# New written orders for the opening and the first feed-forward stage of a macaron block, with earlier halves of the first tiles and later biases

## The chip, the cores and the metric

The kernel runs on one core of one Trainium2 chip. The number that counts is the time of one execution on the device in microseconds (us); the kernel before takes 1006.35 us, the median of three runs (1004.93 to 1006.83). The engines that matter are TensorE (PE, matrix products and transposes; PEld is its weight load), VectorE (DVE), ScalarE (ACT), GpSimd (POOL), and the queue of SyncE (SP), which only issues DMA transfers. Each engine takes its instructions in the order in which they were written; an instruction that has to wait holds up all that stand behind it on its engine.

## The reference

The input is 4096 rows of 256 numbers (2 x 2048 x 256, float32). With `ffn` the quantised feed-forward block, the reference computes

```
x = x + 0.5 * ffn(layernorm(x))
x = x + attention(layernorm(x))
x = x + 0.5 * ffn(layernorm(x))

ffn(x):   gate = q(x) @ q(w_gate).T          # 256 -> 704
          up   = q(x) @ q(w_up).T            # 256 -> 704
          return q(silu(gate) * up) @ q(w_down).T   # 704 -> 256
q(v):     blocks of 16 along the last axis; scale = max(max|block| / 6, 1e-12)
          v / scale rounded to the grid 0, .5, 1, 1.5, 2, 3, 4, 6 (with sign), times scale
attention(x): q, k, v = x @ Wq.T + bq, x @ Wk.T + bk, x @ Wv.T + bv   (512 wide)
          softmax(q k.T / 16) v @ Wo.T + bo, for each of the two sequences of 2048 rows
```

All inputs and the output are float32. The weights of the feed-forward block are quantised in the kernel too, and they are the same for both feed-forward blocks.

## The kernel before

The 4096 rows are 32 tiles of 128 rows, kept on chip in four groups of eight tiles (`xs`, 1 MB each). The kernel has an opening, the first feed-forward stage (FFN0), attention, and the second feed-forward stage (FFN1). Products come in pieces: for tile i, `p{i}` is gate product (PE), silu (ACT), up product (PE), and gate times up (DVE); `b{i}` is the product with w_down (PE) and its addition to x (DVE).

**Opening** (`opening`). It loads the weights and the first group of x, quantises w_gate and w_up in two halves each (`g0 g1 u0 u1`, function `half`) and w_down in two (`d0 d1`, function `down`), folds the projections of attention into two matrices (`f`, function `fold`), measures the layer norms of the first two groups (`n0 n1 n2`), normalises and quantises tiles 0 to 11 in pairs (`x0` to `x5`), makes the products of tiles 0 to 7 (`p0` to `p7`), quantises their hidden rows in pairs (`h0` to `h3`), turns four of these tiles with PE (`t0` to `t3`) and takes them back (`b0` to `b3`). A quantisation is a chain over three engines: DVE takes the largest of each block, scales and inverts it; POOL or DVE multiplies; ACT takes absolute values; DVE rounds in two instructions (lines 426 and 428); POOL or DVE multiplies back (line 430).

Each of these activities is a generator, and each `yield` ends one step. The string `ORDER` lists 261 steps by name; the function `opening` runs them in just that order, and `fence` then ties the instructions of each engine to that order. The planner has no freedom left there: where a name stands in the string decides what stands ahead of it on PE, DVE, ACT, POOL.

**FFN0** (`woven`) is written in the same way by `FFN0_ORDER` (503 steps) for tiles 8 to 31. Here a quantised tensor is turned by a DMA transpose instead of PE. For a pair of hidden tiles, `h{i}` is DVE and ACT work, then a transposing DMA (line 259, SP queue), then one multiplication on POOL (line 261). `s{i}` brings the scales: one PE transpose (`ts`, line 272), an ACT copy (`whole`), a DMA that lays them out (`eight`, line 278), and a DMA that spreads them over the target tile (`hqT<-eight`, line 281). `x{i}` and `y{i}` are the same for four input tiles (`xqT<-eight`). There is a single buffer `eight`: the next line-278 transfer waits until the line-281 transfer before it has landed. All of these are issued by the SP queue in written order. `n3`, `m0`, `m1` are further layer norm statistics, `a0` to `a7` turn the rows of the first sequence for attention, `q` makes its first scores, `t4` to `t7` turn the last hidden tiles of the opening. Attention and FFN1 follow; their order is not touched.

Buffers that the steps share: PE's gate and up products have two PSUM buffers (`p_big`), the products `b{i}`, the weight transposes and the scores have two (`p_acc`). So a new product waits until ACT or DVE has read an older one.

**Loads.** The ACT queue issues the first four tiles of x as one transfer of 512 KB (line 148) and the four biases; the SP queue issues w_gate rows, wq, the other w_gate rows, wk, w_up, wv, wo, the other four tiles of x, w_down, and the remaining groups of x (lines 162 to 187). A row of w_gate is 1 KB; `load_rows` puts row r*128+p on partition p.

## Time and profile before

| | |
|---|---|
| time, median of three runs | 1006.35 us |
| time of the profiled execution | 1006.27 us |
| span of its trace (first to last instruction) | 1004.5 us |
| TensorE clock granted | 1.0 throughout |
| busy: PE / DVE / ACT / POOL | 979.8 / 797.1 / 416.7 / 409.3 us |
| first instruction of DVE on data | 6.17 us |
| first gate product | 30.0 us |
| opening ends (last `b3` addition on DVE) | about 92 us |
| FFN0 ends, attention goes on alone | about 326 us |

The span is split into engines' busy times; an instruction of PE that overlaps the next one is counted to its modelled end, so the idle times between PE rows are better read from the starts of the rows: a gate or up product is eight rows of 0.296 us each from start to start (2.37 us), a product with w_down twelve rows of 0.216 us (2.59 us). Times in the trace count from the start of the span.

### The profile page before, as it was taken

To read this page: it belongs to the slowest core of one execution; us is meant where nothing else is said; L and a number is where in the kernel's file an instruction comes from. 1 tells how busy PE (TensorE), PEld (TensorE's weight loads), DVE (VectorE), ACT (ScalarE), POOL (GpSimd) and SP (SyncE) were. 2 spreads that over 40 slices of the span, in tenths; PEclk is the share of its full clock that TensorE was granted. 3 is DMA by queue.
4 is the path that set the end of the run, shared out by engine and by line. 5 is a ranking of instruction groups with operands and counts; after the bars stand their busy time and mean duration, and the time that the engine had idled before them with its cause. 6 is when DMAs were issued, how large, how long until landed. Compare 5 with 4: busy or idle time off the path is not lost.

```text
span 1004.5 us, 11698 instructions
## 1 busy us (share of the span) xinstructions
PE 979.8 (98%) x4137; PEld 750.0 (75%) x4137; DVE 797.1 (79%) x1324; ACT 416.7 (41%) x745; POOL 409.3 (41%) x451
## 2 busy tenths in 40 slices
PE   5999999999999999999999999999999999999998
PEld 3667766767766888888888888888765666776776
DVE  7999999979753798665688858677978389988896
ACT  4755543343333534353544444343654244233121
POOL 4465132331124595566665555556411102133231
PEclk9999999999999999999999999999999999999999
DMA  9001255442430000000000000000000033665553
GB/s 310 28 1 40 56 113 94 96 106 55 90 88 2 0 1 1 1 1 1 1 1 1 1 1 1 1 1 1 0 1 1 10 79 99 127 136 109 123 115 75
DMA packets 59294, 49.40 MB, mean 49 GB/s; under 512 B 46050, under 2 KB 51171, under 8 KB 58851
## 3 DMA queue, kind: packets, MB, share of 16 engines
q1 hardware_dynamic: 58272, 48.11, 21.3%
q10 hardware_dynamic: 962, 0.53, 0.3%
q8 instruction: 33, 0.54, 0.2%
q14 instruction: 27, 0.21, 0.1%
HBM read 8.46 MB, written 4.19 MB: 13 GB/s over the span
## 4 chain that ended last, share of the span: by engine, by line
PE 80%; DVE 15%; ACT 2%; issue 1%; DMA 1%; SPq 0%; ACTq 0%; DVEq 0%
PE gu L591 23%; PE m L1153 16%; PE ps L1256 13%; PE po L647 12%; PE poa L1202 3%; PE pu L970 3%; PE ps L1224 2%; PE z L1172 2%; PE ps L1016 2%; DVE h L252 2%; PE ps L1033 1%; DVE qh_s L233 1%; PE th L632 1%; DVE h L609 1%; DMA wq_sb<-in_wqT_dram 1%
## 5 line engine op out<-in xcount | busy, mean ns | idle before, releaser
L591 PE MATMUL gu<-wgu,xqT 128*128 128x352 f32 x992 | 306.2, 460 | 2.7 <-issue 0.8
L591 PEld LDWEIGHTS gu<-wgu,xqT 128*128 128x128 f32 x992 | 185.3, 190 | 101.1 <-issue 5.9
L647 PE MATMUL po<-wd,hqT 128*128 128x256 f32 x768 | 174.0, 380 | 0.0
L647 PEld LDWEIGHTS po<-wd,hqT 128*128 128x128 f32 x768 | 144.1, 190 | 26.3 <-issue 2.7
L261 POOL TENSOR_TENSOR hqT<-hqT,qh_t 128x1408 f32<-128x1408 f32 x24 | 74.6, 3109 | 194.7 <-DMA qh_t<-h 154.0
L1153 PE MATMUL m<-st,xn 128*128 128x256 f32 x448 | 132.9, 379 | 0.0
L1256 PE MATMUL ps<-uT,xS 128*128 128x256 f32 x432 | 127.3, 379 | 0.0
L1153 PE MATMUL m<-tw,xn 128*128 128x256 f32 x336 | 99.9, 379 | 0.0
L1128 POOL TENSOR_TENSOR tw<-st 128x256 f32<-128x256 f32 x55 | 46.3, 841 | 129.9 <-PE m L1153 62.0
L1153 PEld LDWEIGHTS m<-st,xn 128*128 128x128 f32 x448 | 84.5, 190 | 11.3
L1256 PEld LDWEIGHTS ps<-uT,xS 128*128 128x128 f32 x432 | 80.9, 190 | 10.9
L605 ACT ACTIVATE h<-gu 128x704 f32<-128x704 f32 x62 | 46.7, 756 | 99.2 <-PE gu L591 95.2
L609 DVE TENSOR_TENSOR h<-h,gu 128x704 f32<-128x704 f32 x62 | 54.3, 878 | 35.0 <-PE gu L591 29.0
L1109 DVE TENSOR_TENSOR st<-st,top 128x1024 f32<-128x1024 f32 x64 | 76.5, 1210 | 2.8 <-PE top L1104 2.7
L1113 ACT ACTIVATE st<-st 128x1024 f32<-128x1024 f32 x64 | 66.7, 1058 | 11.7 <-DVE st L1109 11.5
L1153 PEld LDWEIGHTS m<-tw,xn 128*128 128x128 f32 x336 | 63.8, 190 | 8.6
L1233 DVE TENSOR_TENSOR most<-st,most 128x512 f32<-128x512 f32 x49 | 39.4, 803 | 32.3 <-ACT st L1274 32.3
L1256 PE MATMUL ps<-uT,xT 128*128 128x256 f32 x216 | 64.4, 380 | 0.1
L261 POOL TENSOR_TENSOR xqT<-xqT,qx_t 128x1024 f32<-128x1024 f32 x9 | 20.3, 2258 | 104.9 <-DMA qx_t<-qx_q 62.8
L1266 ACT COPY st<-ps 128x256 f32<-128x256 f32 x54 | 20.1, 373 | 98.6 <-PE ps L1256 98.6
L249 ACT ACTIVATE qh_m<-h 128x1408 f32<-128x1408 f32 x24 | 33.0, 1376 | 56.7 <-DVE h L244 36.9
L1130 POOL TENSOR_TENSOR tw<-st 128x256 f32<-128x256 f32 x55 | 50.0, 910 | 4.3
(234 smaller groups left out, 1625.9 us busy)
## 6 DMA issues: line engine op xcount, KB each, us to landing
hqT<-eight SPq DMA_DIRECT2D x24, 704.0 KB
...
```

The lines of the kernel that those rows point to most:

```text
L261: nc.gpsimd.tensor_tensor(state["dst"], state["dst"], crossed, ALU.mult)
L591: nc.tensor.matmul(out=ps[:, b2, 0:HALF], lhsT=xqT[:, i % XT, kc, :], rhs=wgu[:, kc, ts(which * 2 + b2, HALF)], start=(kc == 0), stop=(kc ...
L605: nc.scalar.activation(h, gate, AF.Silu)
L609: nc.vector.tensor_tensor(h, h, up, ALU.mult)
L647: nc.tensor.matmul(out=po, lhsT=hqT[:, r, :], rhs=right, start=(k == 0), stop=(k == NR - 1))
L1109: nc.vector.tensor_tensor(piece, piece, top, ALU.subtract)
L1113: nc.scalar.activation(piece, piece, AF.Exp, scale=SCALE)
L1128: add(t[:, 0, :], b[:, 0, :], b[:, 1, :], ALU.add)
L1130: add(t[:, 1, :], b[:, 1, :], b[:, 0, :], ALU.add)
L1153: i = nc.tensor.matmul(out=gr.m[k], lhsT=left, rhs=right, start=first, stop=last)
L1233: nc.vector.tensor_tensor(gr.most, piece[:, 1, :], gr.most, ALU.max)
L1256: nc.tensor.matmul(out=out, lhsT=left, rhs=right, start=start, stop=stop, skip_group_check=True)
```

## The change

Four things are changed.

1. `ORDER` and `FFN0_ORDER` hold the same steps in another order. Nothing is added or taken from either.
2. The first four tiles of x come in two transfers of two tiles each, both on the ACT queue.
3. The first halves of w_gate and w_up are loaded with three rows after each other on a partition (3 KB in one piece, row 3p+r on partition p) instead of rows 128 apart; the ACT copies of those halves into `wgu` write with a stride of three to put the columns back. w_up is loaded in two halves and its last rows.
4. The biases leave the ACT queue for the SP queue: bq and bk behind w_gate, bv behind w_up, bo behind w_down. bv is loaded as four rows of 128 numbers, and PE and ACT turn it into a column (one transpose into a `p_big` buffer and one copy), where POOL copied it before.

The choice of one of two buffers in `turned` (attention's rows) was by a count of calls and is now by a fixed list; the list gives the same buffers to the same p as the count did in the order before.

```diff
@@ -33,25 +33,25 @@
 
 
 FFN0_ORDER = """
-t5 x12 n2 n3 x12 x12 n2 n2 n2 m0 t5 x12 x12 n2 p8 p8 t4 x12 t4 n3 n2 x12 n3 p9 y12 n2 p9 p8 y12 m0
-n2 n3 n2 x12 y12 n2 n2 p9 p8 x12 n2 x12 y12 p9 t7 t7 n3 b5 h8 n2 n3 h8 n3 h8 t6 p10 h8 s8 p10 x12
-x12 n2 n2 n2 p11 h8 p11 t6 x16 h8 x16 h8 b5 n3 x16 m0 p11 x16 n3 x16 p11 m0 s8 b4 p10 p10 b7 h10 h10
-n3 b4 x12 p12 s8 x16 s10 x16 p12 m0 x16 h10 s10 h10 n3 p13 p12 p13 s8 x16 s10 p13 x16 h8 p12 p13 y16
-p15 n3 x16 h10 n3 h10 b7 x20 b6 x20 p14 h12 h12 b6 s10 h10 x16 s12 h8 x20 x20 m0 m0 m0 m0 x20 y16
-h12 y16 x20 y16 x20 s12 x20 b9 p15 m0 h10 p14 h12 p15 x16 p14 b9 b8 p14 p15 s12 h14 h14 y20 x20 n3
-m0 p17 h12 h12 s12 p16 h12 h14 p17 s14 b8 m1 h14 p16 s14 p16 n3 p16 h14 h10 p17 s14 n3 h14 p17 s14
-x20 h12 y20 y20 b11 b11 x20 m0 p19 p19 p18 h12 h16 h16 x24 m0 p18 h14 s16 m0 x24 s16 h16 y20 x20 b10
-p19 x24 x24 p18 b12 x20 p19 m0 s16 h16 m0 b10 b13 h16 a1 h14 x24 p18 a0 x24 p20 h14 a0 h18 h18 a1
-s16 b12 s18 m1 s18 x24 a0 p20 a0 m1 p21 s18 h16 x24 b13 h18 p21 x24 m1 h16 y24 p21 h16 p20 p21 p20
-x24 m1 a1 s18 h18 b14 h18 p23 h20 y24 h20 a1 x24 m1 y24 h18 b15 h20 p22 p23 b14 m1 h16 h18 p23 h20
-p22 s20 b16 x24 x28 y24 s20 h18 x24 p23 p22 b15 h20 b17 p24 p22 m1 m1 h18 h22 h20 s20 h22 p25 m1 s20
-x28 p24 m1 b16 h20 p25 s22 p24 s22 h20 h22 p25 x28 b17 h22 s22 h20 x28 x28 x28 a3 a3 a2 q y28 p24
-p25 h22 b20 b20 x28 a2 p26 s22 m1 x28 a2 y28 x28 h22 h22 a3 a2 y28 y28 h24 b18 b19 m1 h24 b18 h22
-x28 b19 x28 p26 a3 p27 x28 p27 h24 p27 h24 p26 m1 p27 m1 p26 m1 s24 s24 x28 h26 b21 a4 p28 p29 h26
-h24 a4 s26 p28 h22 s24 h24 h26 a4 h24 p28 h26 s26 h24 b22 s24 a4 p28 p29 s26 b21 p29 p29 p31 h28 p30
-h26 p30 h28 p31 s28 a7 s26 h26 a5 h28 b23 a7 p31 a5 a7 h24 h28 a7 h26 p31 s28 b23 p30 h26 a5 s28 b22
-a6 b24 p30 a6 h28 h28 b24 h30 a6 q s28 a5 h28 q h30 a6 q s30 h26 h30 b27 h30 s30 h28 b27 b25 h28 b25
-h30 s30 h30 q h30 b28 s30 h30 b29 b28 h30 b29 q b30 b31 b30 b26 b31 b26
+p8 p8 n2 p9 t4 t5 m0 n2 p9 x12 p9 n2 p8 x12 x12 n2 x12 x12 x12 t4 p8 t5 x12 n2 b5 n3 y12 t7 n2 n3
+x12 y12 p9 n2 y12 n2 n3 n2 h8 p10 x12 n2 x12 h8 h8 n2 n2 n3 n3 t7 t6 n2 p11 b7 p10 x12 p10 p11 n2 n2
+n2 h8 s8 y12 x16 m0 x16 b7 x12 p10 m0 p11 s8 t6 m0 x12 s8 b4 p11 h8 h8 x16 h10 p12 x16 p12 h10 x16
+x16 h10 p13 h8 p13 b4 h10 b5 s10 p13 p13 s8 s10 x16 h10 x16 p12 h10 s10 p12 x16 h12 y16 p14 y16 n3
+b6 m0 b6 p15 x16 h8 m0 h12 p14 s10 y16 y16 p14 h12 s12 h8 x16 p15 m0 x16 m0 p14 h10 p15 p15 b9 x20
+x20 x20 x20 h14 b8 x20 h10 n3 s12 n3 x16 h14 p16 m0 h10 x20 b8 m0 h14 p17 y20 m1 h12 x20 p16 h12 p17
+s12 h12 n3 h12 n3 s14 s14 p16 b10 s12 p18 m0 b9 p16 n3 h14 h14 s14 p17 m0 h12 y20 n3 x20 n3 p18 x20
+p17 h16 s14 x20 x20 h16 b11 n3 b11 n3 n3 y20 x20 h12 b10 p19 m0 h14 p19 x24 x24 h16 p19 m0 m1 y20
+s16 m1 s16 x24 p18 h14 s16 h16 p19 p18 b13 h14 m0 x20 h18 h18 h16 b12 x24 x24 p20 m1 x24 s18 h16 p20
+h18 b13 b12 p21 h18 h14 p21 p21 x24 m0 x24 s18 b14 p20 x24 p21 m1 s16 a0 s18 h16 p20 b15 s18 x24 h16
+b15 p23 y24 h18 p23 a0 x24 h16 h20 x28 p23 a0 p22 y24 h20 h18 b14 x24 m1 a1 h20 x28 y24 a1 s20 p23
+h18 x28 y24 p22 h20 b16 a0 s20 a2 b16 m1 p22 p22 s20 x28 x28 a1 x24 h22 h22 x28 m1 h18 h20 a1 a2 x28
+h18 s20 q m1 a3 p25 h22 s22 q s22 m1 m1 h20 h20 p24 b17 h22 s22 p25 b18 p24 a3 h22 b17 h22 p25 p25
+p24 p24 m1 b19 h24 s22 h20 x28 b19 p27 x28 h24 m1 p27 b18 y28 p26 p26 m1 h20 x28 h22 x28 y28 a3 b21
+m1 y28 x28 s24 p27 h24 s24 y28 b20 h24 p26 m1 a3 b20 p27 a4 h22 a4 a2 a7 h24 p26 h22 h26 x28 h24 a4
+a7 h26 h24 b23 h26 a2 h26 p28 p29 p28 p28 b23 p29 p29 h24 p28 s24 p31 s24 s26 a4 h26 a5 p29 s26 p31
+p30 s26 b21 q b22 a7 h28 p30 p30 h28 h26 s28 h28 s26 a7 b22 h24 a6 h28 b24 s28 p31 h26 h28 b24 h28
+h26 p30 q h26 a6 h28 p31 q h30 b27 s28 s28 h30 s30 h28 a5 h30 s30 b27 h28 s30 b25 s30 h30 b28 b25 a6
+a5 b29 h30 h30 h30 h30 b28 a5 b29 q h30 b26 b31 b26 b30 a6 b30 b31
 """
 FFN1_ORDER = """
 n2 h6 n2 t5 t4 p8 t4 t5 h6 n3 p9 h6 s6 p8 n2 p9 n2 n3 s6 n3 p9 n2 p8 n2 n2 n2 h6 p9 n2 p8 n3 h8 p10
@@ -74,14 +74,14 @@
 b30 h31b t31 t31 b30 b29 b31 b29 b31
 """
 ORDER = """
-n0 n0 n0 g0 g0 g0 g0 n0 n0 g0 n0 g1 n0 g1 n0 f n0 g1 g0 n0 f g0 f n0 g1 n0 g0 g1 x1 u1 x0 f x1 u0 x0
-g1 f u0 g0 u1 g1 f f x0 x1 g1 u0 x0 n1 u1 g1 n1 u0 x0 n1 x0 f x1 n1 n1 u1 x1 n1 d1 u0 u1 x1 u0 n2 g1
-f n1 n2 n1 u1 x0 d1 g1 f n1 x0 x1 x0 n1 u1 g0 x0 n1 x1 g0 p0 n1 x3 u1 u0 x2 p1 u1 n2 p0 d0 u1 x3 x1
-u0 u0 x3 d0 d1 n2 d0 d1 d1 u1 p1 n2 x2 n2 u0 n2 x3 u0 x2 d0 x3 x1 n2 x3 x2 n2 p0 x3 x2 n2 d1 x2 d0
-n2 p0 d0 n2 x3 n2 p1 p3 x2 p1 f n2 x2 n2 d0 h0 p3 d1 d0 h0 n2 p2 d1 p2 h0 x3 x4 x3 p3 x4 h0 x4 p3 p2
-x2 p2 x4 x5 x5 h1 d0 x2 x5 p6 p4 x4 h0 h0 p6 p5 h1 x4 h0 p4 d1 x4 h0 x4 h1 p5 p4 p5 h1 h0 h1 x5 p4
-d0 p5 p7 x4 h1 h2 d1 t0 p7 d1 x5 h1 x5 h2 t0 h1 p6 x5 p6 h2 h2 t1 p7 h1 h2 p7 h3 x4 d0 t1 x5 h2 b0
-h3 t2 h3 x5 h3 t2 h2 b1 b0 t3 x5 h2 t3 h3 b1 h3 h3 b2 h2 h3 b3 b2 b3 h3
+n0 n0 g0 g0 g0 n0 g0 n0 n0 n0 g1 g1 n0 g0 g1 n0 n0 f f g1 u0 g0 n0 u0 u0 n0 g0 n0 f g1 u0 u0 g0 g1
+g1 u1 n1 f n1 x0 g1 x1 x0 f n1 u1 n1 x0 g1 n1 u1 u0 u1 n1 x1 f d0 f g0 u1 n2 f x0 n1 x0 u0 n1 x0 x0
+n1 f x0 u1 f g0 n1 d0 x0 u0 g1 x0 g0 n1 g1 u1 n1 d1 u0 x1 n2 x1 x3 p1 p1 u0 n2 x1 u1 x1 n2 u0 p0 d1
+d0 u1 x3 x2 d1 x1 x1 n2 d0 d1 x1 u1 n2 n2 x3 x2 n2 x2 u1 d0 n2 p0 p1 n2 p1 x2 x1 d0 p0 f x3 n2 p3 d1
+p0 d1 x2 n2 p3 d1 d0 x3 x2 x2 n2 p2 x3 p2 p2 x2 n2 h0 x2 n2 x3 x2 x3 x3 n2 p2 h0 x4 d0 x5 d1 p3 x3
+p4 h0 d0 d0 h0 h0 p3 p4 h0 x4 p6 p6 x4 p5 d0 x5 h1 x5 h1 x4 d1 x4 h0 h0 p5 h1 p5 p5 h0 p4 x4 p6 x5
+t0 h1 p4 h2 h2 h1 t1 x4 p7 x5 h1 x4 t1 h2 h1 d1 d1 x4 x4 p7 t0 h1 p6 b1 x5 h1 p7 t2 b1 x5 h2 p7 h3
+h3 x5 h2 x5 h3 h3 t2 b0 b0 t3 b2 h2 h2 h2 h3 t3 h3 h3 b3 h2 h3 b2 b3 x5 h3
 """
 TURNED = 4
 
@@ -145,7 +145,8 @@
 
 
     xs = [const.tile([P, GT, D], FP, tag=f"x{g}", name=f"x{g}") for g in range(NG)]
-    nc.scalar.dma_start(out=xs[0][:, 0:4, :], in_=x_g[0][:, 0:4, :])
+    nc.scalar.dma_start(out=xs[0][:, 0:2, :], in_=x_g[0][:, 0:2, :])
+    nc.scalar.dma_start(out=xs[0][:, 2:4, :], in_=x_g[0][:, 2:4, :])
     w_nat = []
     for name in ("gate", "up"):
         t = wpool.tile([P, NR, D], FP, tag=f"n_{name}", name=f"n_{name}")
@@ -165,24 +166,30 @@
             nc.sync.dma_start(out=t[0:LAST, NR - 1, :], in_=w[(NR - 1) * P:FF, :])
 
     NH = NR // 2
-    load_rows(w_nat[0], w_gate, 0, NH)
+    bq_sb = wpool.tile([P, KE], FP, tag="bq", name="bq_sb")
+    bk_sb = wpool.tile([P, KE], FP, tag="bk", name="bk_sb")
+    bv_sb = wpool.tile([KE, P], FP, tag="bv", name="bv_sb")
+    bo_sb = wpool.tile([P, D], FP, tag="bo", name="bo_sb")
+
+    def load_next(t, w):
+
+        nc.sync.dma_start(out=t[:, 0:NH, :], in_=w[0:NH * P, :].rearrange("(p r) k -> p r k", p=P))
+
+    load_next(w_nat[0], w_gate)
     nc.sync.dma_start(out=wq_sb, in_=wqT.rearrange("(k p) e -> p k e", p=P))
     load_rows(w_nat[0], w_gate, NH, NR)
+    nc.sync.dma_start(out=bq_sb, in_=bq)
+    nc.sync.dma_start(out=bk_sb, in_=bk)
     nc.sync.dma_start(out=wk_sb, in_=wkT.rearrange("(k p) e -> p k e", p=P))
-    load_rows(w_nat[1], w_up, 0, NR)
+    load_next(w_nat[1], w_up)
+    load_rows(w_nat[1], w_up, NH, NR)
+    nc.sync.dma_start(out=bv_sb, in_=bv.rearrange("(c p) -> c p", p=P))
     nc.sync.dma_start(out=wv_sb, in_=wvT.rearrange("(k p) e -> p k e", p=P))
     nc.sync.dma_start(out=wo_sb, in_=woT.rearrange("(k p) e -> p k e", p=P))
     nc.sync.dma_start(out=xs[0][:, 4:GT, :], in_=x_g[0][:, 4:GT, :])
     nc.sync.dma_start(out=wd_nat, in_=w_down.rearrange("(r p) k -> p r k", p=P))
-    bq_sb = wpool.tile([P, KE], FP, tag="bq", name="bq_sb")
-    bk_sb = wpool.tile([P, KE], FP, tag="bk", name="bk_sb")
-    bv_sb = wpool.tile([P, KE], FP, tag="bv", name="bv_sb")
-    bo_sb = wpool.tile([P, D], FP, tag="bo", name="bo_sb")
     nc.gpsimd.memset(bo_sb[P - 32:P, :], 0.0)
-    nc.scalar.dma_start(out=bq_sb, in_=bq)
-    nc.scalar.dma_start(out=bk_sb, in_=bk)
-    nc.scalar.dma_start(out=bv_sb, in_=bv.rearrange("(c p) -> p c", p=P))
-    nc.scalar.dma_start(out=bo_sb[P - 1:P, :], in_=bo.unsqueeze(0))
+    nc.sync.dma_start(out=bo_sb[P - 1:P, :], in_=bo.unsqueeze(0))
     for g in range(1, NG):
         nc.sync.dma_start(out=xs[g], in_=x_g[g])
 
@@ -440,9 +447,11 @@
             ps = weight_bank([P, 4, P], f"wt{which}_{half}_{kc}")
             for r in range(NH):
                 nc.tensor.transpose(ps[:, r, :], t[:, half * NH + r, ts(kc, P)], ident)
-            nc.scalar.copy(
-                wgu[:, kc, ds(which * FF + half * NH * P, n)], ps.rearrange("p r k -> p (r k)")[:, 0:n]
-            )
+            to = wgu[:, kc, ds(which * FF + half * NH * P, n)]
+            if half == 0:
+                nc.scalar.copy(to.rearrange("q (p r) -> q r p", r=NH), ps[:, 0:NH, :])
+            else:
+                nc.scalar.copy(to, ps.rearrange("p r k -> p (r k)")[:, 0:n])
             yield
 
     def down(r):
@@ -477,8 +486,12 @@
                 nc.scalar.activation(
                     nat[name][:, c0 + c, 0:D - 1], ps[:, c, 0:D - 1], AF.Identity, bias=last[:, c:c + 1]
                 )
-            if c0 == 0:
+            if c0 == 0 and bias.shape[0] == P:
                 nc.gpsimd.tensor_copy(nat[name][:, :, D - 1], bias)
+            elif c0 == 0:
+                turned = p_big.tile([P, 2, 512], FP, tag="big", name="bias")[:, 0, 0:KE]
+                nc.tensor.transpose(turned, bias, ident[0:KE, 0:KE])
+                nc.scalar.copy(nat[name][:, :, D - 1], turned)
 
         def matrix(dst, left, right, kc):
             ps = weight_bank([P, D], f"wm{kc}")
@@ -854,7 +867,7 @@
     PLAIN = NP + LAG
     groups = NT // QG
 
-    kept, turns = {}, {"nat": 0}
+    kept = {}
 
     def ones_last(pool, tag, k, shape, last):
 
@@ -882,8 +895,7 @@
 
         def turned(self, p, kt):
 
-            turns["nat"] += 1
-            if turns["nat"] % 2:
+            if p in ((1, 3, 4, 5), (0, 2, 4, 6))[self.b]:
                 nat = ones_last(xp, "xl", None, [P, 4, D], lambda t: t[:, :, D - 1])[:, 0:2, :]
             else:
                 nat = ones_last(kt, "nat", 0, [P, 2, D], lambda t: t[:, :, D - 1])
```

## The prediction

> **What bounds the kernel now.** Read first: the page's busy tenths in 40 slices, then the busy times by stretch (PE, PEld, DVE, ACT, POOL, granted clock, DMA share, GB/s).
>
> ```profile
> PE   5999999999999999999999999999999999999998
> DVE  7999999979753798665688858677978389988896
> ```
>
> ```profile
> 0.00:30.00 30.00, 17.21 (x72) 12.85 (x72) 23.26 (x69) 16.24 (x40) 12.88 (x22) 1.00 0.81 282
> 30.00:92.00 62.00, 59.99 (x262) 42.84 (x263) 59.62 (x99) 36.21 (x60) 37.20 (x19) 1.00 0.03 7
> 92.00:175.00 83.00, 80.03 (x312) 55.77 (x310) 79.19 (x140) 36.08 (x56) 19.45 (x9) 1.00 0.45 86
> 326.00:700.00 374.00, 373.86 (x1765) 325.73 (x1764) 281.06 (x548) 166.65 (x347) 227.64 (x319) 1.00 0.00 1
> ```
>
> After 326 us PE works without holes for 374 us, so what PE gains earlier reaches the end. Up to 92 us it is DVE that has no idle time: 59.62 of 62 us, and 23.26 of the 23.83 us from its first row on. Then the timeline (start, length, engine, line, what; in brackets the idle time before and its releaser):
>
> ```profile
> 6.17 1.08 DVE L331 BATCH_NORM_STATS2 bn<-x 128x6 f32<-128x256 f32 x3 [6.17 <-DMA x<-in_x_dram]
> 7.16 0.94 DVE L408 TENSOR_REDUCE qw_s<-n_gate 128x48 f32<-128x768 f32 x1
> ...
> 30.00 5.00 PE L591 MATMUL gu<-wgu,xqT 128*128 128x352 f32 x16 [0.35 <-ACT xqT L524]
> ```
>
> PE's first product starts at 30.0. Its holes after that, from the starts of its rows less 0.296, 0.216 or 0.110 us for a row of 352, 256 or 128 columns, where over 0.25 us: 1.36 (at 36), 0.69 (43), 0.46 (83), 1.09 (95), 0.60 (136), 0.71 (142), 0.92 (148), 0.47 (166), 0.48 (214), 0.26 (283), together 7.0. So 7.0 us of holes and the wait up to 30 us are all there is to win. Two of the holes:
>
> ```profile
> 43.49 0.83 PE L591 MATMUL gu<-wgu,xqT 128*128 128x352 f32 x2 [0.52 <-DVE sd L349]
> ```
>
> ```profile
> 95.74 0.27 PE L272 MATMUL ts<-ident,qx_p 128*64 128x128 f32 x1 [0.93 <-ACT h L605]
> ```
>
> The second is a transpose of scales that stands on PE ahead of products and waits for DVE (`x12` scales). Last, the SP queue in FFN0:
>
> ```profile
> 124.09 0.72 SPq L278 DMA_DIRECT2D eight<-whole  x1
> 124.90 2.51 SPq L259 DMA_TRANSPOSE qh_t<-h  x1
> 127.51 0.64 SPq L281 DMA_DIRECT2D hqT<-eight  x1
> ...
> 135.59 0.66 SPq L278 DMA_DIRECT2D eight<-whole  x1
> 137.52 0.64 SPq L281 DMA_DIRECT2D xqT<-eight  x1
> ...
> 143.85 0.71 SPq L278 DMA_DIRECT2D eight<-whole  x1
> ```
>
> A spread of scales holds the one `eight` buffer from its issue to its landing: 8.1 us for a hidden pair (127.51 to 135.59), 6.3 us for four input tiles (137.52 to 143.85). With 2.0 us for `eight` itself, these steps have a pace of 8.3 to 10.1 us that no order can shorten.
>
> **How I cost an order.** Both orders hold the same steps, so the sums of work are equal. What differs is how much DVE work stands ahead of what PE waits for. For each PE group I add, in written order, the durations of the DVE rows up to the end of what the group waits for, and the PE rows ahead of it (PE by start to start: gate or up 2.37, `b` 2.59, transposes 0.110 each, rows of the fold by their lengths). DVE minus PE is the lead that PE must leave to DVE. Rows: reduction over 768/512/1024/1408 columns 0.94/0.66/1.20/1.60, rounding 0.95/0.68/1.22/1.62, h times up 0.87, statistics 0.41.
>
> Before, the largest leads are: `p2` gate waiting for `p1`'s multiplication 43.7-28.0 = 15.7; `p6` gate for `p3` 52.8-36.0 = 16.8; `x12` scales 90.0-76.2 = 13.8; `p15` 16.1; `p17` 16.6; `h16` scales 162.3-143.8 = 18.5. After: `p2` gate 40.0-28.0 = 12.0; `p6` gate 52.9-38.8 = 14.1; `p7` up 72.2-58.2 = 14.0; `x12` scales 89.2-83.5 = 5.7; `p14` 10.8; `p17` 11.3; `h16` scales 10.9; the largest of FFN0 `h18` scales 172.2-158.8 = 13.4. I call "lost" PE's clock less its sum of work: before, 30.0-14.4 = 15.6 at the first product, plus 7.0 in holes, plus 0.4 of small ones, 23.0 at the end.
>
> **The opening.** DVE's work ahead of the first product falls from 24.7 (pair `x0` multiplied back) to 23.5, which is 1.0 us at its pace there (22.45 us of clock for 24.7 of sum). Its start: of x's 512 KB the first half now lands by itself, so two of the statistics go ahead of w_gate's reduction; the third comes behind. In exchange the reduction must wait for w_gate itself, which the row at 7.16 shows not waiting; SP's next issue shows it landed by 7.07 (a wait of 0.3 us). If w_gate's first half lands at 6.2 (no bias packets beside it), DVE is 0.5 us ahead; at 7.1 it is 0.3 us behind. I take 0.3 ahead, nearer the earlier landing, since packets on ACT's queue fall from 962 to 256. ACT has two copies more ahead of that product (`g0` and `g1`, 0.48 and 0.42) and costs it 0.3. First product 30.0-1.0-0.3+0.3 = 29.0, lost 14.6. Then `u1` weights: DVE ends its rounding at about 32.5, POOL multiplies (2.08 in the row of before) to 34.7, while PE is ready at 34.1: +0.6. From there the leads of 14.0 to 14.1, with DVE's clock 1.6 to 2 us behind its sum (p5's multiplication before: 66.9 against 64.9), ask for lost of 15.7 to 16.1. I take 16.0 at 75 us, where before has 17.7.
>
> The strided copy of the first weight halves: no row of before has a stride. Lower end 0 (0.42 to 0.48 us as now), upper end twice the row, four copies, 1.9 us, of which at most two stand ahead of the first product, 1.0 us. I take 0, because PE's transposes and the POOL step bound both sides. Biases: the turn of bv is one transpose (0.110) and one ACT copy (0.2 like line 475's 0.16) in place of POOL's 0.19; both stand in PE's idle time before 29 us, and with `p_big` not yet in use. Moved issues: ACT loses four of 0.45 to 0.88 us, in time when it waits for x (first use 10.67); it gains one. SP gains four of some 0.5 us; bq and bk leave by about 3.8, before the wait that follows. This row shows what limits SP:
>
> ```profile
> SPq L165 <- DMA x<-in_x_dram: 3.9, 1, 3.9
> ```
>
> The ninth transfer (x, four biases and three on SP are out) waits for the first to land. After, the first eight are x twice, w_gate three times with wq among them, bq and bk; wk waits for x's first half only, w_up for its second. wk leaves at about 4.5 instead of 7.07, w_up at about 6 instead of 8.52. By the volumes of before (about 370 KB a microsecond after 6 us) w_up's first half lands at 11.4, DVE asks for it at about 12.6; the second half of x lands by 16.5, DVE asks at 17.8. Cost 0, with covers of 1.2 and 1.3 us.
>
> The Trainium skill speaks against the split: "DMA: Bandwidth & Descriptors", Measured, advises transfers of 1 MB or more, and its Anatomy section gives each transfer a fixed 2 us or so. Should the second half pay that anew, it would land near 8.2 and hold DVE, which asks for it at about 7.5, 0.7 us; the forecast would be 0.7 us later. Against it stand SP's issues, 0.5 us apart at 0.74 and 1.27, whose data flow together; the sum goes by these.
>
> **FFN0.** DVE leads fall from 15 to 18.5 down to 6 to 13.4, so eight of the ten holes lose their cause. What is late next is the SP queue. Before, from the scales of `h10` on PE (121.62) to the end of POOL's multiplication of `x16` (146.08) it takes 24.5 us. After, PE has 126.8-104.4 = 22.4 us of work between these; the ACT copy waited 2.0 us in that chain, which the new order may or may not take away: a hole of 0 to 2.1. For `x20` the spread now stands behind the transpose (2.4 us of issue), from `h14`'s scales 23.0+2.4 = 25.4 us against 24.8 of PE work, plus what the queue is already late: 0 to 2. I take 2.0 for both, and 0.5 for small holes elsewhere; the later chains (`h18` to `h30`) have 2 us and more of cover. Lost at the end 16.0+2.0+0.5 = 18.5 against 23.0: 4.5 us gained. The profiled execution is 1006.27 (span 1004.5 and 1.8 around it), the median 1006.35, 0.1 above: 1006.35-4.5 = **1001.8 us**, span about 1000.
>
> **Rivals.** (a) *The crossing takes most of it back.* The spreads' pace of 8.3 to 10.1 us binds PE from `x16` to `x20`, and further to `h16`; holes of 4 to 6 us instead of 2, gain 0.5 to 2.5, 1003.9 to 1005.9. For it: SP waits of up to 8.2 us for a spread. Against: before keeps PE at 0.9 us of holes with the same pace. (b) *Slower by the loads.* bq and bk now run on SP's ring between w_gate and wk, 256 packets; before, the biases issued from 1.2 to 3.8 had packets until 8.9. If they hold up the ring 4 us each, w_up and x come 8 us later, DVE stalls 8 less 1.2 of cover, and the stall passes to PE whole, since DVE has no idle time to 92 us: 1001.8+6.8 = 1008.6. It decides from 4.5+1.2 = 5.7 us of delay on. Against: in the records of the transfers their packets took 9 ns each. (c) *Nothing changes*: the leads fall, but DVE, 95% busy from 92 to 175 us, stalls on POOL's and ACT's order instead, and lost ends at 22 to 24: 1005.3 to 1007.3. (d) *All holes close*: lost 16, 999.3.
>
> **How the numbers follow.** Runs of this kernel tell 0.2% (2 us) from no change. Chances: forecast with (d), 999 to 1003.9, 0.70; (a) 0.14, of which 0.04 is faster by over 0.2%; (c) 0.08; (b) and other losses 0.08. Faster 0.70+0.04 = 0.74; same 0.10+0.06 = 0.16; slower 0.08+0.02 = 0.10. The range leaves out (b) and the worse half of (c): 998.8 to 1006.0.
>
> **What would show it.** Right: DVE's first row near 4 to 5 us; first product at 28.5 to 29.5; `ts` transposes of scales without a hole before them; PE holes of some 3 us between 30 and 326 us; attention starting alone about 321.5. Wrong: DVE waiting for `n_gate`, `n_up` or `x` after 7 us; PE waiting at `p16` or `p20` for POOL's line 261 over 2 us; first product after 30; a hole at `u1`'s transposes over 1.5 us.

## The result and the profile after

The changed kernel takes 1018.20 us (median of 4 runs, 1017.92 to 1019.07) against 1005.89 us before in the same comparison (4 runs): 1.0124 times the time before, interval 1.0106 to 1.0141. The forecast was 1001.8, range 998.8 to 1006.0: wrong in sign. The profiled execution is 1019.07, its span 1017.2.

The stretches of the changed kernel (PE, PEld, DVE, ACT, POOL, granted clock, DMA share, GB/s):

```profile
0.00:30.00 30.00, 16.61 (x54) 13.10 (x55) 24.59 (x62) 13.61 (x34) 11.85 (x21) 0.89 0.78 282
30.00:92.00 62.00, 59.57 (x262) 41.94 (x262) 61.11 (x100) 34.36 (x59) 30.75 (x17) 1.00 0.00 1
326.00:700.00 374.00, 373.19 (x1739) 320.14 (x1738) 278.51 (x547) 167.79 (x349) 228.91 (x336) 1.00 0.00 1
```

DVE is busier than before in the first two (24.59 and 61.11 us against 23.26 and 59.62), yet PE gets no more done: 54 rows against 72 up to 30 us, then 262 in both. PE's granted clock is 0.89 up to 30 us, where it was 1.00: it is 0.5 from 22.24 to 29.07 us, a stretch that begins inside a hole of 4 us. DVE's first rows and PE's first product:

```profile
5.04 0.75 DVE L338 BATCH_NORM_STATS2 bn<-x 128x6 f32<-128x256 f32 x2 [5.04 <-DMA x<-in_x_dram]
5.71 0.94 DVE L415 TENSOR_REDUCE qw_s<-n_gate 128x48 f32<-128x768 f32 x1
...
32.97 1.75 PE L604 MATMUL gu<-wgu,xqT 128*128 128x352 f32 x5
```

DVE starts 1.1 us sooner than before (6.17) and reduces w_gate 1.45 us sooner (7.16). PE's first product is nevertheless 3.0 us later (30.00). PE's clock less its sum of work, the "lost" of the prediction, is 3.1 us more than before at 75 us, 2.4 more at 125, 6.4 more at 210 and 11.7 more at 270. The first row of attention behind FFN0 (`m`) starts 12.9 us late, and from there the distance stays (12.6 at PE's last row). So PE loses some 3 us in the opening and nearly all the rest behind 150 us. PE's longest waits from 92 to 345 us:

```profile
PE po L660 <- POOL hqT L268: 3.8, 1, 3.8
PE gu L604 <- POOL xqT L268: 1.4, 1, 1.4
PE gu L604 <- DVE h L622: 1.1, 1, 1.1
```

Before, in the same part, the longest single wait was 0.9 us.

**DVE's rows got longer.** In the changed kernel, DVE and then POOL in the opening:

```profile
14.66 0.95 DVE L435 SCALAR_TENSOR_TENSOR n_gate<-qw_m,n_gate 128x768 f32<-128x768 f32 x1
15.53 2.25 DVE L433 SCALAR_TENSOR_TENSOR n_gate<-qw_m,n_gate 128x768 f32<-128x768 f32 x1
...
31.87 1.49 DVE L365 TENSOR_TENSOR shift<-least,rstd 128x4 f32<-128x4 f32 x1
```

```profile
14.82 2.14 POOL L425 TENSOR_TENSOR n_up<-n_up,qw_r 128x768 f32<-128x768 f32 x1 [1.73 <-DVE qw_r L423]
...
31.15 2.19 POOL L437 TENSOR_TENSOR n_up<-n_up,qw_s 128x768 f32<-128x768 f32 x1 [5.17 <-DVE rstd L362]
```

A rounding of 768 columns takes 0.95 us, but 2.25 where it starts during POOL's multiplication (14.82 to 16.96): its own 0.8 to 0.95 us begin when POOL ends. A row over four columns, 0.15 us elsewhere, takes 1.49 beside POOL's row from 31.15 to 33.34. It holds in both directions: a POOL multiplication of 768 columns takes 1.49 us alone (at 11.60) and 2.14 here, where DVE's rounding from 14.66 has 0.79 us left when it starts.

I call the time of a DVE row above what the same line and shape usually takes (the lower quartile of its times in the two kernels) its *stretch*. I count, over both kernels up to 340 us, the rows that start at least 0.1 us behind the start of a POOL multiplication and 0.2 us or more before its end, and call those with over 0.1 us of stretch stretched. Rounding and multiplying with both tensors in SBUF (scalar_tensor_tensor 19 of 20, tensor_tensor 14 of 17) and tensor_scalar (23 of 27) are stretched; tensor_reduce (0 of 23), the statistics (0 of 83), reciprocals (0 of 16) and rows with one input in PSUM, such as L622 and L662 (0 of 34), are not. Of 332 rows of the first kinds that start at other times, 4 are, each of which starts within 0.1 us of POOL's multiplication. The stretch also has a size: in 50 of the 56 it is the time that was left of POOL's multiplication less 0.13 us, to within 0.05. Five of the other six are one line of eight rows (`qh_r`) most of which are held, so that the quartile is no measure of its usual time.

The sum of stretch over 0.15 us up to the addition of the fourth tile's product with w_down to x (L662, in the tables below "fourth addition") is 7 us before and 16 after. That addition, DVE's last of the opening, ends at 92.05 before and 100.25 after: 8.2 us, nearly the difference in stretch.

The Trainium skill has this rule: "SBUF — State Buffer", section "Who interferes with whom", gives VectorE and GpSimd one shared port pair, taken as a whole for the length of an instruction, against tensor_scalar in its two-port modes and against instructions with two SBUF inputs while GpSimd reads SBUF; tensor_reduce never. The counts above agree. The prediction had not used this rule.

**Steps stand behind others.** The rows of the 3.8 us wait, in the changed kernel: first DVE, then SP, then POOL and PE.

```profile
235.13 1.63 DVE L259 SCALAR_TENSOR_TENSOR h<-qh_m,h 128x1408 f32<-128x1408 f32 x1 [1.17 <-ACT qh_m L256]
...
241.18 3.30 DVE L251 SCALAR_TENSOR_TENSOR xl<-xl,qx_r 128x1024 f32<-128x1024 f32 x1
...
246.75 1.62 DVE L263 SCALAR_TENSOR_TENSOR h<-qh_m,h 128x1408 bf16<-128x1408 f32 x1
```

```profile
247.08 0.66 SPq L285 DMA_DIRECT2D eight<-whole  x1
249.53 1.23 SPq L266 DMA_TRANSPOSE qx_t<-qx_q  x1
250.81 0.64 SPq L288 DMA_DIRECT2D xqT<-eight  x1
251.55 3.85 SPq L266 DMA_TRANSPOSE qh_t<-h  x1
```

```profile
258.39 2.85 POOL L268 TENSOR_TENSOR hqT<-hqT,qh_t 128x1408 f32<-128x1408 f32 x1 [14.99 <-DMA qh_t<-h]
...
261.30 4.47 PE L660 MATMUL po<-wd,hqT 128*128 128x256 f32 x12 [3.84 <-POOL hqT L268]
```

Pair h22's first rounding ends at 236.8; its second begins at 246.75, because two products, h24's reduction and x28's multiplication (stretched to 3.30) were written ahead of it. Its transposing transfer then stands on SP behind three transfers of x28, which are needed later. PE waits, a hole of 4.0 us between its rows, and then the granted clock is 0.50 from 261.18 to 264.59 us (0.93 over 250 to 275, 1.00 before): six rows stand 0.43 us apart instead of 0.216, and the twelve take 4.47 us where they take 2.75 at the full clock. Hole and slow rows together are 5.7 us.

### The profile page after: what moved, and what is told of

It reads as the page before. It is cut to its first block, busy times and chain, and to the rows that moved or that the text cites. A ratio compares the mean times of both kernels' runs of the same rounds, so it can differ in the third digit from the quotient of the medians.

```text
span 1017.2 us, 11718 instructions
## 1 busy us (share of the span) xinstructions
PE 984.8 (97%) x4138; PEld 753.1 (74%) x4138; DVE 806.2 (79%) x1324; ACT 417.5 (41%) x746; POOL 401.7 (39%) x450
## 4 chain that ended last, share of the span: by engine, by line
PE 72%; DVE 21%; issue 2%; DMA 2%; ACT 2%; POOL 0%; SPq 0%; ACTq 0%; POOLq 0%; DVEq 0%
PE gu L604 18%; PE m L1165 16%; PE ps L1268 13%; PE po L660 9%; PE poa L1214 3%; PE pu L982 3%; DVE h L259 2%; PE ps L1236 2%; PE z L1184 2%; PE ps L1028 2%; DVE h L251 2%; DVE qh_s L240 1%; DVE h L263 1%; PE ps L1045 1%; DVE h L622 1%
## 5 line engine op out<-in xcount | busy, mean ns | idle before, releaser
L268 POOL TENSOR_TENSOR hqT<-hqT,qh_t 128x1408 f32<-128x1408 f32 x24 | 70.9, 2954 | 224.3 <-DMA qh_t<-h 171.1
L1165 PE MATMUL m<-tw,xn 128*128 128x256 f32 x336 | 99.9, 379 | 0.0
L622 DVE TENSOR_TENSOR h<-h,gu 128x704 f32<-128x704 f32 x62 | 54.2, 876 | 33.2 <-PE gu L604 21.5
L1125 ACT ACTIVATE st<-st 128x1024 f32<-128x1024 f32 x64 | 66.7, 1058 | 11.7 <-DVE st L1121 11.4
```

The lines of the kernel that those rows point to most:

```text
L268: nc.gpsimd.tensor_tensor(state["dst"], state["dst"], crossed, ALU.mult)
L622: nc.vector.tensor_tensor(h, h, up, ALU.mult)
L1125: nc.scalar.activation(piece, piece, AF.Exp, scale=SCALE)
L1165: i = nc.tensor.matmul(out=gr.m[k], lhsT=left, rhs=right, start=first, stop=last)
```

## The experiments

Theory P: the loss is DVE held while POOL reads SBUF, because the new order puts more sensitive rows beside POOL's. Theory O (called F in the first expectations where it concerns FFN0): the order itself, which makes needed steps stand behind others in queues kept in order. A third: the loads. A later one, Q, is theory O for SP's queue with its one buffer `eight`. The letters stand in the expectations too; L is there the loads in E1 to E4, and from E10 on the rival that POOL's lateness is the cost.

### E1 to E4: one part at a time

E1 is the changed kernel with the old `ORDER`, E2 with the old `FFN0_ORDER`, E3 with both old (the new loads alone), E4 the kernel before with both new orders and the old loads. In E4 the alternate buffers of attention's rows follow the old count, which changes part of what attention reads: only its time counts.

> The changed kernel with the opening's order put back; the new loads and the new order of FFN0 stay. Theory P (the loss is made in the opening, where VectorE's rows were stretched by 16.0 us behind GpSimd's running multiplications, against 7.3 before, and everything later is the echo of it): faster than before, 1001 to 1005, first product at 29 to 30. Theory F (the new order of FFN0 makes the holes after 150 us by itself, 11.8 us more than before between 150 and 350 us): 1013 to 1018 with a normal opening, holes of over 3 us near 255 us again.

> The changed kernel with FFN0's order put back; the new loads and the new opening stay. Theory P: 1012 to 1018, first product at 33 as in the changed kernel, VectorE some 8 us later at the opening's end than before. Theory F: 1006 to 1010, only the 3 us by which the first product is later, and less of it at the end.

> Before with only the new loads (x in two transfers, three rows to a partition, biases on SyncE's queue); both old orders. Both theories: VectorE's first row about 1 us earlier, and then 1004.5 to 1006.5. A theory L, that the loads themselves cost time (late w_up, strided copies, bias turn): 1008 or more, with VectorE waiting for a transfer after 6 us.

> Before with only the two new orders; the old loads. Both P and F: 1016 to 1020, as the changed kernel or up to 1.5 us later, since VectorE starts at 6.2 and not at 5.0. Theory L: 1006 or less.

| | opening | FFN0 | loads | us | ratio, interval | fourth addition | start of attention alone, against before |
|---|---|---|---|---|---|---|---|
| E1 | old | new | new | 1016.11 | 1.0105 (1.0090 to 1.0120) | 92.3 | +10.7 |
| E2 | new | old | new | 1013.91 | 1.0080 (1.0065 to 1.0095) | 99.9 | +7.8 |
| E3 | old | old | new | 1005.30 | 1.000 (0.9991 to 1.0010) | 92.3 | -0.6 |
| E4 | new | new | old | 1020.58 | 1.0143 (1.0126 to 1.0160) | 102.0 | +15.5 |

Under the old orders the loads together cost and gain nothing (1005.30 against 1005.46): the third theory falls. Under the new orders they gain 2.4 us (E4 against the changed kernel), and E4 lies 0.6 above its expectation. Each order costs by itself, 8.6 us the opening (E2 against E3) and 10.8 the stage (E1 against E3), and both together 12.9, less than their sum: a stage that will wait anyway takes up part of a late opening. From the changed kernel, the old opening alone takes back 2.1 us and the old stage alone 4.3. E1's opening is the old one, and yet PE waits from 137 us on in the same places, 4.0 us for h22 among them. So the stage has a loss of its own, which P in the opening can't explain.

### E5: h22's two steps sooner

In the order of the stage, `h22`'s second rounding right behind its first, its transposing transfer ahead of y28's and x28's:

```
-... h22 b17 h22 p25 p25 p24 ... x28 h22 x28 y28 ... a4 h22 a4 ...
+... h22 b17 h22 h22 p25 p25 p24 ... h20 h22 x28 x28 y28 ... a4 a4 ...
```

> The changed kernel with two steps of one pair moved: the second rounding step of h22 on DVE (L263) stands right behind the first (L259) instead of behind two products' multiplications, h24's reduction, x28's first multiplication and a batch of small rows; and h22's transposing transfer stands ahead of x28's and y28's transfers in SP's queue. Theory O (the order makes a needed step stand behind others in a queue that is kept in order): the 4.0 us hole of PE at 257 us, which ends on POOL's multiplication of hqT, goes, and with it the five po rows at half clock behind it (666 against 379 ns, 1.4 us); PE is solid after it, so 4 to 5.5 us reach the end: 1012.7 to 1014.5. Rival D (DVE is simply full there, so that what is done sooner makes another row late): the hole comes back within 20 us as a wait for x28 or h24, and the time stays at 1016.5 to 1019. Theory P (DVE rows held while POOL multiplies) says nothing of it: the same rows collide, within 1 us.

1012.62 us (1011.82 to 1015.53), 5.6 less than the changed kernel; 1.008 of before. In E5:

```profile
246.47 3.68 POOL L268 TENSOR_TENSOR hqT<-hqT,qh_t 128x1408 f32<-128x1408 f32 x1 [3.72 <-DMA qh_t<-h]
```

h22's second rounding stands at 236.08 instead of 246.75, POOL has h22 at 246.5 instead of 258.4, PE has no hole over 0.3 us between 186 and 309, and its clock in 250 to 275 is 1.00. The gain of 5.6 us is the hole and the slow rows of before (5.7). O holds for this wait.

### E6, E7: POOL's multiplications cut short

```
-nc.gpsimd.tensor_tensor(yb, yb, by_block(rec), ALU.mult)
+nc.gpsimd.tensor_tensor(yb[:, 0:1, :], yb[:, 0:1, :], by_block(rec)[:, 0:1, :], ALU.mult)
```

and the same for the multiplication back, with the new opening (E6) and the old (E7), both with the old order of the stage. The rest of these multiplications is left out of the computation, so the time alone counts.

> The new opening, with the old order of the feed-forward stage, and POOL's multiplications in the opening (both lines of Rounding) cut to the first block of 16 columns: the rounded weights and activations of the opening then lack those multiplications, and the time alone counts. POOL's rows fall from 1.5 to 2.6 us each to about 0.2. Compared with its pair, the old opening cut in the same way. Theory P (DVE rows that read two tensors of SBUF are held until POOL's row ends, and the new order puts 8.7 us more of them beside POOL): the stretch of DVE rows in the opening goes from 16.0 to under 2 us, the four adds of the first tiles end within 2 us of the pair's, and the two times within 2 us: about 1000 to 1004. Theory O (the order itself makes DVE, ACT and PE wait for each other in turn): these adds end 5 us or more behind the pair's, and the time stays 5 us or more above it: 1006 to 1010.

> The pair of the run before: the old opening and the old feed-forward order with the new loads, POOL's multiplications in the opening cut to the first block of 16 columns in the same way (left out of the computation as there). DVE loses 7.3 us of stretch before 92 us, where it was the bound; by P and by O alike the four adds then end at 84 to 90 instead of 92.3, and the time is 999 to 1004. What the two theories differ on is how far the new opening with the same cut lies above this run: within 2 us by P, 5 us or more by O.

E6 1003.90 (ratio 0.9986, 0.9977 to 0.9995), E7 1001.80 (0.9968, 0.9957 to 0.9979). The distance of the openings falls from 8.6 us to 2.1. DVE's stretch in the opening is 0.2 us in E6 and nothing in E7, the fourth addition ends at 89.3 and 87.5. And without stretch E6's first product stands at 28.40, 1.2 ahead of E7's: the lead that the prediction had counted. By the 256th product's row both are level, and at 212 us E6 has a hole of 1.0 us that E7 lacks; the runs don't show where the lead of 1.2 us goes.

### E8: the new order of the stage for its first half alone

> Old opening, new loads, and a feed-forward order that is the new one up to the end of tile 23's multiplication (about 203 us) and from there the old one, less the steps already done. Where the new feed-forward order loses its time: with the old opening it made holes of 6.3 us of PE between 100 and 205 us, against 2.4 of the old order, and 5.7 against 0.3 after that. By Theory O each hole belongs to the order of its own stretch: the first 3.9 us are lost here, the rest not: 1008 to 1010.5, with no hole of 4 us after 205. If instead what the first half leaves undone is what is missing in the second, the 4 us hole or its like stays, and the time is 1013 to 1016. If the first half's holes are later made good, 1004.5 to 1006.5.

1010.01 us (1008.55 to 1011.31; 1.0045, 1.0030 to 1.0060). The holes up to 205 us stay (0.9, 1.1, 2.2, 1.6), the large one is absent. With E5: some 5 us of the stage's loss are made before 205 us, the rest behind it, nearly all at h22.

### E10, E13, E14: POOL as late, but with short instructions

Short multiplications also bring POOL's results sooner. Here POOL is kept busy with fills of a spare tile between two short multiplications; E10 and E13 have the new opening, E14 the old, all with the old order of the stage. The edit of E13 and E14 (E10 has 128 for 96, with a larger tile):

```
-nc.gpsimd.tensor_tensor(yb, yb, by_block(rec), ALU.mult)
+nc.gpsimd.tensor_tensor(yb[:, 0:1, :], yb[:, 0:1, :], by_block(rec)[:, 0:1, :], ALU.mult)
+for _ in range((n - 256) // 96):
+    nc.gpsimd.memset(self.spare, 0.0)
+nc.gpsimd.tensor_tensor(yb[:, 1:2, :], yb[:, 1:2, :], by_block(rec)[:, 1:2, :], ALU.mult)
```

> The new opening with the old order of the feed-forward stage, and each of POOL's multiplications of the opening done for two blocks of 16 columns only (the rest of them is left out, the time alone counts), the first before and the second after a row of fills of a spare tile that keep POOL busy for about as long as the whole multiplication took. POOL is as late as in the new opening, but fills read nothing. Theory P (DVE's rows are held by POOL's reads of SBUF): stretch of DVE rows in the opening under 4 us instead of 16, the four adds done by 92, time 1003 to 1006. Rival L (what the short multiplications gave was only that POOL's results came sooner): adds done at 97 to 100 and 1009 to 1013. If fills hold DVE as well, the stretch says so: 12 us or more, and the time is as with L.

E10: 1009.73 us (1.0040, 1.0026 to 1.0055). DVE's stretch is 0.1 us at most and the fourth addition ends at 90.8, as P expects; the time is as L expects. The profile says why: ACT's copy into `hqT` waited 5.4 us for the last fill of the spare tile, whose memory `hqT` takes over. E13 and E14 have the tile elsewhere.

> The new opening with the old feed-forward order and POOL's multiplications as two short ones around fills, as in the earlier run with fills, but with the spare tile in memory that nothing takes over later: there the copies of hqT had to wait 5.4 us for the last fill, which made PE holes of 4.6 us at 90 to 95 us that belong to the experiment alone. DVE's rows were not stretched by the fills (0.1 us against 16) and the four adds were done at 90.8. Theory P: that again, no hole over 2 us at 90 to 95, the time 1002.5 to 1005.5, and within 3 us of its pair, the old opening with the same fills. Rival L (POOL's lateness is the cost): 5 us or more above the pair.

> The pair: the old opening and the old feed-forward order, with the same short multiplications and fills. Its DVE rows lose the 7.7 us of stretch that they have in the opening, and POOL is about as late as before: adds done at 87 to 90, time 1001.5 to 1004.5 by both theories. The distance of the new opening above it decides: within 3 us by P, 5 us or more by L.

E13 1004.03 (0.9978, 0.9969 to 0.9988), E14 1003.30 (0.9980, 0.9970 to 0.9989): 0.7 us apart, where the same two openings with POOL's full multiplications are 8.6 apart (E2, E3). DVE's stretch is 0.5 us or less in both. POOL's chains take about as long as its multiplications did: for 768 columns 1.32 us against 1.49, for 1408 columns 2.8 against 2.6 (POOL is busy 26.96 us in E13's stretch of 30 to 92, 30.77 in E2's). The fourth additions still stand 3.3 us apart (92.3 in E13, 89.0 in E14; 7.5 in E2 and E3), but little of that reaches the end. The row of 2.25 us and its POOL neighbours in E13:

```profile
14.77 0.97 DVE L438 SCALAR_TENSOR_TENSOR n_gate<-qw_m,n_gate 128x768 f32<-128x768 f32 x1
```

```profile
14.07 0.86 POOL L427 TENSOR_TENSOR n_up<-n_up,qw_r 128x16 f32<-128x16 f32 x1 [1.75 <-DVE qw_r L425]
14.87 0.99 POOL L429 MEMSET spare<- 128x64 f32 x5
15.81 0.22 POOL L430 TENSOR_TENSOR n_up<-n_up,qw_r 128x16 f32<-128x16 f32 x1
```

0.97 us beside fills, 2.25 beside the multiplication; the short multiplication ahead of them (0.22 alone) is itself held to 0.86 by DVE's rounding. So the opening's loss is P: not POOL's being busy or late, but DVE's sensitive rows held for the length of POOL's multiplications. That it is the reading which holds them is argued, from the skill's rule, and not shown: a fill reads nothing, but it is also only 0.15 to 0.20 us long, and by the 0.13 us above it could stretch a row by no more than 0.07. Of 27 rows of tensor_scalar that start inside a fill, three with 0.16 to 0.20 us of it left are longer by 0.03 to 0.07 us, as if they were held. No run has a long instruction of POOL that reads nothing beside DVE.

### E12: the square root behind the copies

The 3.9 us hole in PE's fold at 20 us in the changed kernel has ACT's square root of the second norm standing ahead of the copy of `wa`. It is moved behind it.

> The changed kernel with one step moved: the square root of the second norm (ACT, L351) stands behind the copies of wa and the first half of v's turning instead of ahead of the second copy of wa, where it waited 5.5 us for the variance that DVE had late. If the order of ACT's queue is a cause of its own: PE's hole of 3.9 us at 20 us goes, the first product comes 1 to 2.5 us sooner (30.5 to 32), and the adds of the first tiles, which hang on DVE, come 0 to 1 us sooner, so that the time is 1016.5 to 1018.5. If the late variance is all there is (P), the first product is within 0.5 us of 32.97 and the time within 0.7 us of 1018.2.

1018.42 us (1018.22 to 1020.63). The hole goes from there and comes back 4 us later (4.1 us at 23.8, for w_gate's transposes); the first product is at 32.19, 0.8 sooner, between the two expectations, and the 64th product's row is 0.2 sooner. Nothing of it reaches the end, so the order of ACT's queue is no cause of its own here.

### E9, E11, E15, E16, E18: the 2.3 us hole at 180 us

In E5, PE waits 2.28 us at 180 for POOL's multiplication of x20, whose last operand was y20's second transfer. It stood behind s14's, as one buffer `eight` serves all. E9 is E5 with y20's three steps (its copy into `whole`, its transfer to `eight`, its spread) ahead of s14's, E11 is E9 with the old opening.

```
-... s14 s14 ... s14 ... y20 ... s14 ... y20 ... y20 ...
+... s14 ... s12 y20 y20 y20 s14 ... s14 ... s14 ...
```

> The changed kernel with h22's two steps sooner, as in the run before that did this, and with y20's three steps after its transpose (copy, transfer to eight partitions, transfer to all) ahead of s14's on ACT and SP. In that run PE waited 2.28 us at 180 us for POOL's multiplication of xqT; its last operand was y20's transfer, which stood on SP behind s14's (5.8 us of waiting for the one buffer of eight). Theory O: the hole goes, with five products' rows at half clock behind it, and 2 to 3.5 us reach the end: 1009 to 1010.6. Rival D (DVE is full between 100 and 200 us, 0.3 to 1.0 us idle, so the hole only moves): the sum of PE's holes between 100 and 205 us stays within 0.7 us and the time is 1012 to 1013.

> The run with h22's and y20's steps sooner, with the old opening in place of the new one. The old opening alone was worth 2.1 us under the feed-forward order as changed (1016.1 against 1018.2). With the two large holes gone the stage has less room to take up a late opening, so more of the opening's 7.8 us should show: Theory O with P: 1004 to 1007, level with the kernel before or up to 2 us off. If the holes only move (rival D): 1010 to 1012.

E9 1016.62 (1.0106), E11 1014.20 (1.0081): E9 is 4 us worse than E5, and both lie outside what either theory expected. In E9:

```profile
168.52 0.71 SPq L285 DMA_DIRECT2D eight<-whole  x1
169.34 1.40 SPq L266 DMA_TRANSPOSE qh_t<-h  x1
...
173.04 1.28 ACT L618 ACT_TABLE_LOAD   x1 [7.38 <-DMA qh_t<-h]
```

s14's first transfer waits for the one buffer until 168.5, h12's transposing transfer behind it leaves 7.7 us later than in E5, so the buffer of `h` is free later, ACT's silu waits 7.4 us (the row at 173.04 is the first of its work) and PE 4.8. E15 puts h12's transfer between y20's two and s14's behind; E16 is E15 with the old opening; E18 also has x20's transposing transfer ahead of s14's second.

> The changed kernel with h22's steps sooner, and y20's transfers sooner in another way than in the run that failed: there h12's transposing transfer was left standing behind s14's first transfer, which waits for the one buffer of eight, and so released the buffer of h 7.7 us late, and PE waited 4.9 us at 170. Here y20's first transfer is followed by h12's transposing transfer, then by y20's second, and s14's two come after that. Theory Q (SP's queue with its one buffer of eight is a chain in order, and who stands where in it decides which product waits): no hole over 1.5 us at 168 to 185, and 2 to 3.5 us less than 1012.6: 1009 to 1010.6. If s14, now 8 us later, is what the next product waits for: a hole of 2 us or more before 215 and 1012 to 1015.

> The run before with the old opening: new loads, old opening, new feed-forward order with both repairs. By P and Q together it is 1.5 to 4 us under that run: 1006 to 1008.5, near the kernel before. If a late opening still disappears in the holes of the stage, it is within 1.5 us of it.

> The run with y20's transfers between and h22's sooner, with one step more: x20's transposing transfer ahead of s14's second transfer (704 KB) in SP's queue. In that run y20's transfer was in by 170, but POOL's multiplication of x20 still began only at 181.9, 8.6 us after x20's transposing transfer was issued at 173.3 behind s14's. Theory Q: that transfer lands before 177, POOL multiplies at 176 to 178, the hole of 2.3 us at 182 and the half-clock rows behind it go, 1.5 to 3.3 us less than 1014.05: 1010.8 to 1012.5. If DVE's rows are what sets x20 back, the hole stays at 1.5 us or more and the time is 1013 to 1015.

E15 1014.05 (1.0079), E16 1010.96 (1.0047), E18 1014.45 (1.0092). All three miss: E15 and E18 lie where their rivals do, E16 is 3.1 us under E15 as expected, but above its range. In E15 the hole stays, 2.3 us: the operand that comes last is now x20's transposing transfer, behind s14's. In E18 POOL has x20 at 174.6 instead of 181.9 and the hole at 180 is under 0.5 us; and then:

```profile
195.05 4.28 SPq L266 DMA_TRANSPOSE qh_t<-h  x1
...
203.68 0.76 ACT L618 ACTIVATE h<-gu 128x704 f32<-128x704 f32 x1 [7.30 <-DMA qh_t<-h]
...
204.98 0.44 PE L908 MATMUL txa<-ident,nat 128*128 128x128 f32 x2 [2.94 <-ACT nat L384]
```

In the changed kernel the same silu:

```profile
203.83 0.76 ACT L618 ACTIVATE h<-gu 128x704 f32<-128x704 f32 x1 [5.00 <-DMA qh_t<-h]
```

It waits for the buffer of `h` that a transposing transfer reads, and that transfer shares SP's queue with a spread of 704 KB issued just ahead of it (at 194.00 in E18). Silu starts at 203.83 in the changed kernel, at 202.71, 203.35 and 203.68 in E5, E15 and E18, wherever PE had been before; in E18 ACT's next rows stand behind it and PE waits 2.9 us. The transfers to `eight` leave at 181.2, 192.0 and 205.7 in the changed kernel and at 181.0, 191.9 and 205.6 in E18. In all four kernels silu follows the transfer that leaves at 180 to 181 us by 22.3 to 23.0 us. So Q is right that a wait goes when its transfer is put ahead (E18 at 180), and wrong on the sum: what PE gains there it loses at 205, and an order can make it worse (E9). That the spreads' own pace, 9 to 14 us from one to the next, is the limit here is argued from these times. The runs don't show an order of the new stage's first half without this loss; a second buffer for `eight` was not tried. Under this stage the old opening is worth only 2.1 to 3.1 us (E1, E11, E16 against their pairs) of its 8.

P is at work in the stage too. First the changed kernel, then E18:

```profile
165.77 2.83 DVE L358 TENSOR_TENSOR sd<-sd,var 128x8 f32<-128x8 f32 x1
168.52 0.88 DVE L622 TENSOR_TENSOR h<-h,gu 128x704 f32<-128x704 f32 x1
```

```profile
165.42 0.16 DVE L358 TENSOR_TENSOR sd<-sd,var 128x8 f32<-128x8 f32 x1
```

POOL's multiplication starts at 165.72 in the one (0.05 ahead of the small row) and at 165.34 in the other (0.08 ahead). Once the row is held 2.7 us, and PE waits 1.1 for the product behind it; once not, and then POOL's multiplication takes 2.97 us instead of 2.86, as if it had been the one to wait. The recorded starts alone don't tell which it will be: in E15 DVE's row starts 0.09 us behind POOL's and is held. E15 has PE's hole (1.28 us, ending at 169.28), E5 and E18 don't.

### E17: ten small rows less in the kernel before

```
-nc.vector.tensor_scalar(scale, scale, 1.0 / 6.0, TINY, ALU.mult, ALU.max)
+nc.vector.tensor_scalar(scale, scale, 1.0 / 6.0 / (BELOW if self.first else 1.0), TINY, ALU.mult, ALU.max)
...
-nc.vector.tensor_scalar(rec, rec, BELOW, None, ALU.mult)
```

> The kernel before, with ten small rows of DVE left out of the opening: where POOL does the first multiplication of a rounding, the factor BELOW is divided into the constant of the scale row instead of being multiplied into the reciprocal by a row of its own (line 411 to 417 of the kernel before); the result differs by a part in four million. These rows take 0.17 to 0.36 us each when nothing holds them, some 1.7 us of DVE together, and three of them stood 0.5 to 1.5 us longer beside a multiplication of POOL, 2.8 us together. Theory P: the adds of the first tiles, bound by DVE, come 1.5 to 4.5 us sooner and 1 to 3 us reach the end: 1002.5 to 1005. If the holds only pass to the next row of DVE that reads SBUF in this way: 0.5 to 1 us, within what can be measured: 1004.8 to 1005.8.

1006.50 us (11 runs; 1.0008, 0.9999 to 1.0017): no gain, and above both ranges, though the second expectation has the mechanism. The small rows' stretch is gone, but everything stands otherwise to POOL, and larger rows are now held in E17:

```profile
12.27 2.23 DVE L425 SCALAR_TENSOR_TENSOR n_gate<-qw_m,n_gate 128x768 f32<-128x768 f32 x1
...
24.19 1.99 DVE L419 SCALAR_TENSOR_TENSOR xl<-xl,qx_r 128x512 f32<-128x512 f32 x1
```

0.95 and 0.68 are their usual times; a third, like the second, takes 1.88 at 39.88. The stretch up to the first product goes from 0.9 to 3.4 us and that product from 30.00 to 31.72, with less work of DVE ahead of it. No version of the full computation was found that beats the kernel before; E3 is level with it.

## Why the prediction was wrong

- **What bounds the kernel**: right. DVE up to 92 us, PE without holes after 326 (373.19 of 374 us again), so that what PE loses reaches the end: 12.9 us at the start of attention alone, 12.6 at the end.
- **The loads**, cost 0: right (E3). The first half of x landed at 5.04 or sooner, DVE waited for no second half. The 0.7 us that the prediction weighed against the split, by a figure that the page gives for transfers issued from GpSimd, do not show, and rival (b), slower by the loads, falls. The prediction's rate of 370 KB a microsecond is high for the stretch it was used in (240 to 294 from 10 to 14 us before), but DVE found w_up's first half landed at 11.4, sooner than it was forecast to ask.
- **DVE's start**, taken 0.3 us ahead: it was 1.1, 1.45 at w_gate's reduction.
- **"How I cost an order"** is the step that failed. It adds DVE rows by their durations of before, as if a row's length did not depend on where it stands. The order is what decides which rows stand beside POOL's multiplications. The first product, forecast 29.0, came at 32.97; with POOL's rows short the same order gives 28.40 (E6). The stretch of 8 to 9 us more by the end of the opening was a term missing from the sum, put at nothing without a reason: the new opening alone costs 8.6 us with it (E2 against E3) and 0.7 to 2.1 without (E13 against E14, E6 against E7). Its evidence lay in the profile of before, where a tensor_scalar row that takes 0.23 us at 52.33 took 1.86 beside POOL, and the usual lengths of rows used in the sum hid it:

```profile
61.51 2.90 POOL L430 TENSOR_TENSOR h<-h,qh_s 128x1408 f32<-128x1408 f32 x1 [4.92 <-DVE h L428]
```

```profile
62.61 1.86 DVE L416 TENSOR_SCALAR qh_r<-qh_r 128x88 f32<-128x88 f32 x1
```

- **The crossing, "I take 2.0 for both, and 0.5 for small holes elsewhere"**: the holes between 137 and 205 us are 6.3 us in the changed kernel, not 2.5. One of them (1.3 us) is P, DVE's small row held at 165.77. The pace of the spreads was named; that ACT's silu waits for the buffers that the transposing transfers in the same queue read was not: silu's wait is 5.0 us at 203.83 in the changed kernel and over 7 in E9 and E18, of which PE sees 1.2, 4.9 and 3.1 us. How much of the 6.3 us an order can avoid stays open.
- **"The later chains (h18 to h30) have 2 us and more of cover"**: h22's had less than none, 4.0 us of hole and 5.6 in all (E5). The leads were counted up to DVE's scales of a pair only; the second rounding and the place in SP's queue, further down the same chain, were not followed.
- **Lost at the end**, 18.5 forecast: 23.0 before plus 12.9, near 36.
- **Rivals**: (c) came nearest, with DVE in stalls on POOL's order, but meant waits for results and not rows held while they run, and gave it no more than 1 us of loss; (a), the crossing, put holes of 4 to 6 us there, and 6.3 were measured; both were priced to end no worse than 1007.3.
